# Moving the inversion of softmax sums, scaling out of PSUM, and finishing output blocks singly in a two-layer attention kernel

## The chip, the cores and the metric

The kernel runs on one core of a Trainium2 chip. The metric is the time of one execution on the device in microseconds (us). Before the change the median of three runs is 2982.2 us (2980.04 to 2982.8). The profile is of one further execution, with a span of 2983.8 us from its first instruction to its last. Five engines work side by side and wait for each other through semaphores: TensorE (PE; its weight loads are shown as PEld), VectorE (DVE), ScalarE (ACT), GpSimd (POOL), and SyncE (SP), which only issues DMA transfers here.

## What is computed

The input x is (8, 512, 32, 32) float32: eight batches of 512 channels and 1024 tokens. Two attention layers follow each other, cut here to what matters:

```python
# layer 0: layer norm, 8 heads of 64 channels, softmax, output projection, residual
xn  = layer_norm(x_flat)
q, k, v = xn @ Wq.T + bq, xn @ Wk.T + bk, xn @ Wv.T + bv          # split in 8 heads
attn = softmax(einsum('bqhd,bkhd->bhqk', q, k) / 8)
out = einsum('bhqk,bkhd->bqhd', attn, v) @ Wo.T + bo + x_flat
# layer 1: group norm (32 groups), one head of 512 channels, projection, residual
h = group_norm(x)
attn = softmax(einsum('bcn,bcm->bnm', q, k) * 512 ** -0.5)         # q, k, v from h
x + einsum('oc,bcn->bon', wp, einsum('bnm,bcm->bcn', attn, v)) + bp
```

The kernel leaves out the subtraction of the maximum in the softmax. It takes exponentials of the raw scores, adds them, and divides the values by the sums afterwards. A check of all sums at the end decides whether a second, general path is run; it is not for these inputs.

## The kernel before

Layer 0 works in pairs of heads for 512 of the queries: 8 pairs a batch. For each pair, TensorE makes scores for 8 tiles of 128 keys, ScalarE takes their exponentials p, VectorE adds the tiles to a sum, and TensorE multiplies p by the values. The scores of pair i+1 are always issued before the values of pair i. [...] Small pieces of work for VectorE and ScalarE are put in a queue by `later`, and `tick` takes one piece out at a time, once per key tile in `values`.

```python
def scores(self, ms):                       # class Pair
    for m in ms:
        s = wide_psum(f"s_{self.tag}_{m}")  # three such buffers
        ...  # two matmuls, one for each head                             (L681)
        nc.scalar.activation(p, s, AF.Exp, scale=1.0 / float(D) ** 0.5)  # (L684)
        ...  # self.sum = p[0] + p[1], then self.sum += p                (L688, L690)

def values(self):
    acc = bank(f"acc_{self.tag}")           # two such banks
    for m in range(NM):
        ...  # two matmuls, one for each head                             (L696)
        tick()
    nc.scalar.copy(self.o, acc)             # (L699)

def end_pairs(two):
    den = bank(f"den_{two[0].tag}")
    for k in range(4):                      # sums over keys               (L705)
        nc.tensor.matmul(den[ts(k, BL), :], ones[:, :BL], two[k // 2].sum[:, ts(k % 2, HB)],
                         start=True, stop=True)
    ...
    def invert():                           # transpose L489, reciprocal L655, check L659
        invert_sums(r, compact(t, den))
    def copies():                           # eight small copies to rows   (L718)
        ...  # nc.scalar.copy(rr[n][...], r[...])
    def scale(n):
        nc.vector.tensor_mul(two[n].o, two[n].o, rden[n])               # (L721)
    later(invert, copies)
    for n in range(2):
        later(lambda n=n: expand(rden[n], rr[n]))                        # (L494)
        later(lambda n=n: scale(n))
```

The loop over pairs, and what follows it (`more` is false in the last batch):

```python
for i, p in enumerate(pairs):
    if i + 1 < len(pairs):
        pairs[i + 1].scores(range(NM))
    ...
    p.values()
    if i in (2, 4, 6):
        end_pairs(pairs[i - 2 : i])
if more:
    k_units, kn = project(f"k{b + 1}", ...)     # keys of the next batch
    k_units[0].step(3)
end_pairs(pairs[-2:])
tick(2)
if more:
    k_units[0].rest()
...
o_units, x1 = project_out(b, wo_now, ob, stats)  # output projection, x_out, y_out, z_out
o_units[0].step(1)
add_operands(ob)                                 # T_o: differences of blocks of o
```

All large products are done block by block in seven multiplications instead of eight. Class `Product` has the seven steps. They accumulate into x, y and z in PSUM; S and T are sums and differences of blocks of the operands. A block that is complete is put in `behind`, and `finish` calls `after` for it:

```python
STEPS = [("11", "11", "x", True), ("12", "21", "z", True), ("S2", "T2", "x", False), ("S1", "T1", "y", True),
         ("S3", "T3", "x", False), ("22", "T4", "z", True), ("S4", "22", "y", False)]
...
        elif i == 1: self.out(0, 0, self.u1, self.z)       # out: VectorE adds u and PSUM (L341)
        elif i == 4: ...  # block (1, 1)
        elif i == 5: ...  # block (1, 0)
        elif i == 6: self.out(0, 1, self.u2, self.y)
        if i in (2, 4, 6):
            self.finish()
```

For the last product of layer 1 (x_o, y_o, z_o), `after` starts the load of the residual, scales, adds and stores:

```python
nc.sync.dma_start(out=xr, in_=self.x1[i, k][:, ts(r, HB)])                             # x1r
nc.vector.tensor_mul(t, t, self.rden[:, ts(k, HB)])                                    # (L860)
nc.vector.scalar_tensor_tensor(t, t, bm[:, oc : oc + 1], xr, ALU.add, ALU.add)         # (L861)
nc.sync.dma_start(out=out[b, ts(oc, P), ts(k, HB)], in_=t)                             # (L862)
```

Of the kernel before, what the change touches and what calls it, by code (L numbers as in the profile page):

```python
# [66 lines left out]
def fast_path(ctx: ExitStack, tc: tile.TileContext, x: bass.AP, vecs: dict, weights: dict, out: bass.AP,  # L67
# [41 lines left out]
    def bank(name):  # L109
        return ps_a.tile([P, HB], F32, tag="a", name=name)  # L110
# [196 lines left out]


    side = deque()

    def later(*work):
        side.extend(work)
# [6 lines left out]
    def until(done):  # L319
        while not done():  # L320
            side.popleft()()
# [5 lines left out]
    class Product:  # L327
# [4 lines left out]
        def __init__(self, tag, a, b, part, shift, dest, banks, after=None):  # L332
            self.tag, self.a, self.b, self.part, self.shift, self.dest = tag, a, b, part, shift, dest
            self.banks = banks
            self.after = after or (lambda i, k: None)
            self.behind = []
            self.pieces = 1
            self.done = 0

        def out(self, i, k, u, ps):  # L340
# [8 lines left out]
        def step(self, n=1):  # L349
            for _ in range(n):  # L350
                i = self.done
                self.done += 1
                a, b, to, opens = STEPS[i]
                until(lambda: a in self.a and b in self.b)
                if opens and not hasattr(self, to):
                    setattr(self, to, self.banks(to))
                self.part(getattr(self, to), self.a[a], self.b[b], opens)
                tick(self.pieces)
                if i == 0:
                    self.u1 = self.copy((0, 0))  # L360
                elif i == 1:
                    self.out(0, 0, self.u1, self.z)
                elif i == 2:
                    self.u2 = self.copy((0, 1))
                elif i == 4:
                    u3 = self.copy((1, 1))
                    self.out(1, 1, u3, self.y)
                    self.u3 = u3
                elif i == 5:
                    if self.shift.twice:  # L370
                        self.u3 = self.copy((1, 0))
                    self.out(1, 0, self.u3, self.z)
                elif i == 6:
                    self.out(0, 1, self.u2, self.y)
                if i in (2, 4, 6):
                    self.finish()

        def finish(self):
# [52 lines left out]
    def plain_shift():  # L431
        return make_shift(lambda u, ps, which: nc.scalar.copy(u, ps))  # L432
# [59 lines left out]
    def expand(t, r):  # L492

        nc.vector.transpose(t.rearrange("p (k i) -> p k i", i=BL), r.unsqueeze(2).to_broadcast((P, r.shape[1], BL)))  # L494
# [167 lines left out]
    class Pair:  # L662


        def __init__(self, b, hf, c, qt, kt, vt, ot):
            self.tag = f"{b}_{hf}_{c}"
            self.hf, self.c, self.vt = hf, c, vt
            self.q = qt[c // 2, hf][:, c % 2, :]
            self.k = [kt[c // 2, k][:, c % 2, :] for k in range(NH)]
            self.p = {}  # L670
            self.sum = None
            if c % 2 == 0:
                ot[c // 2, hf] = block(f"o_{self.tag}")
            self.o = ot[c // 2, hf][:, c % 2, :]

        def scores(self, ms):
            for m in ms:
                s = wide_psum(f"s_{self.tag}_{m}")
                for i in range(2):
                    r = slice(i * D, (i + 1) * D)  # L680
                    nc.tensor.matmul(s[:, ts(i, HB)], self.k[m // 4][r, ts(m % 4, P)], self.q[r, :],  # L681
                                     start=True, stop=True)
                p = big_tile(f"p_{self.tag}_{m}")
                nc.scalar.activation(p, s, AF.Exp, scale=1.0 / float(D) ** 0.5)  # L684
                self.p[m] = p
                if m == 1:
                    self.sum = big_tile(f"sum_{self.tag}")
                    nc.vector.tensor_add(self.sum, self.p[0], p)  # L688
                elif m > 1:
                    nc.vector.tensor_add(self.sum, self.sum, p)  # L690

        def values(self):
            acc = bank(f"acc_{self.tag}")
            for m in range(NM):
                for i in range(2):
                    nc.tensor.matmul(acc[i * D : (i + 1) * D, :], value_of(self.vt, m, self.c * P + i * D, D),  # L696
                                     self.p[m][:, ts(i, HB)], start=(m == 0), stop=(m == NM - 1))
                tick()
            nc.scalar.copy(self.o, acc)  # L699

    def end_pairs(two):

        den = bank(f"den_{two[0].tag}")
        for k in range(4):
            nc.tensor.matmul(den[ts(k, BL), :], ones[:, :BL], two[k // 2].sum[:, ts(k % 2, HB)],  # L705
                             start=True, stop=True)
        t = half_tile(f"dent_{two[0].tag}")
        r = small.tile([P, HB // BL], F32, tag="r", name=f"r_{two[0].tag}")
        rr = [small.tile([P, HB // BL], F32, tag=f"rr{n}", name=f"rr_{pair.tag}") for n, pair in enumerate(two)]
        rden = [half_tile(f"rden_{pair.tag}") for pair in two]  # L710

        def invert():
            invert_sums(r, compact(t, den))

        def copies():
            for n in range(2):
                for j in range(4):
                    nc.scalar.copy(rr[n][ts(j, BL), :], r[ts(2 * n + j // 2, BL), :])  # L718

        def scale(n):  # L720
            nc.vector.tensor_mul(two[n].o, two[n].o, rden[n])  # L721

        later(invert, copies)
        for n in range(2):
            later(lambda n=n: expand(rden[n], rr[n]))
            later(lambda n=n: scale(n))

    def project_out(b, w, ot, stats):

# [22 lines left out]
    class Whole:  # L752
# [90 lines left out]
        def values(self, v):  # L843
            b = self.b
            w = {f"{i + 1}{j + 1}": v[i, j].rearrange("p (m o) -> p m o", o=CB) for i in range(2) for j in range(2)}
            shared = {}

            def unit(r):
                y = {}

                def dest(i, k):
                    if (i, k) not in y:
                        y[i, k] = half_tile(f"y_{b}_{r}_{i}{k}")
                    return y[i, k]

                def after(i, k):
                    t, oc = dest(i, k), 2 * i + r
                    xr = half_tile(f"x1r_{b}_{k}_{oc}")
                    nc.sync.dma_start(out=xr, in_=self.x1[i, k][:, ts(r, HB)])
                    nc.vector.tensor_mul(t, t, self.rden[:, ts(k, HB)])  # L860
                    nc.vector.scalar_tensor_tensor(t, t, bm[:, oc : oc + 1], xr, ALU.add, ALU.add)  # L861
                    nc.sync.dma_start(out=out[b, ts(oc, P), ts(k, HB)], in_=t)  # L862

                return Product(f"o1_{b}_{r}", w, self.p, value_part(r), plain_shift(), dest,
                               banks_of(f"o1_{b}", r, shared), after)

            for n in SLOTS[3:]:
                sum_later(w, n, lambda n: big_tile(f"{n}_vm_{b}").rearrange("p (m o) -> p m o", o=CB), wide)
            return [unit(r) for r in range(2)]

    def all_checks():

        one = small.tile([P, 1], F32, tag="one", name="one")
        nc.vector.tensor_reduce(one, checks[:, : n_checks[0]], mybir.AxisListType.X, ALU.add)
        ps = bank("ps_check")
        nc.tensor.matmul(ps[:, :1], ones, one, start=True, stop=True)
        ok = small.tile([P, 1], F32, tag="ok", name="ok")
        nc.vector.tensor_scalar(ok, ps[:, :1], SUM_LIMIT, None, ALU.is_le)
        nc.vector.tensor_scalar(flag, ok[:1, :], -1.0, 1.0, ALU.mult, ALU.add)


    def bias_of(n):
# [2 lines left out]
    with tc.manual_schedule(engines=ORDERED):  # L885
# [67 lines left out]
        for b in range(B):  # L953
# [7 lines left out]
            for i, p in enumerate(pairs):  # L961
# [10 lines left out]
                    hb = operands(ln.result())  # L972
                    add_operands(hb)
                p.values()
                if i in (2, 4, 6):
                    end_pairs(pairs[i - 2 : i])
            if more:
                k_units, kn = project(f"k{b + 1}", wk_next, bias_of("bk0"), hb, True)
                k_units[0].step(3)
            end_pairs(pairs[-2:])  # L980
            tick(2)
            if more:
                k_units[0].rest()
            wa_now = load_w("a", b)
            ob = operands(ot)
# [40 lines left out]
            until(lambda: whole.summed)  # L1026
            whole.inverse()
            v_units[1].rest()
            if not more:
                all_checks()  # L1030
            if more:
                wv_next, wq_next = load_w("v", b + 1), load_w("q", b + 1)
            o_units = whole.values(vm)
            for u in o_units:
                u.step(2)
            for u in o_units:
                u.rest()
            until(lambda: not side)
# [389 lines left out]
```

## Time and profile before

| what | value |
| --- | --- |
| median of three runs | 2982.2 us |
| span of the profiled execution | 2983.8 us |
| mean granted TensorE clock | 0.995 of full speed |
| exponentials of layer 0 (L684) | 512 x 1054 ns on ScalarE |
| adds to the sums (L690) | 384 x 1225 ns on VectorE |
| copies of acc (L699) | 64 x 586 ns on ScalarE |
| copies to rows (L718) | 256 x 202 ns on ScalarE |
| expanding transposes (L494) | 64 x 708 ns on VectorE |
| scaling of o (L721) | 64 x 690 ns on VectorE |

A group's mean is the time of one instruction alone[...]. The "idle before" of a group is time in which its engine had nothing to do just ahead of such an instruction, and the name behind the arrow is what ended it. Idle time of an engine that bounds nothing costs nothing. Ends of matmuls are modelled, so the starts of the instructions say more of TensorE than its busy share does. An "x32" in the chain counts passes of matmuls and weight loads, not matmuls of the program.

### The profile page before, as it was taken

The numbers are of one execution on the slowest core, as the hardware profiler recorded it, in microseconds if no ns is written. First come the engines' busy times: TensorE is split into PE (matmuls) and PEld (weight loads), VectorE is DVE, ScalarE is ACT, GpSimd is POOL, SyncE is SP. The second block draws the span as 40 slices with busy tenths as digits, with TensorE's granted clock in tenths as the row PEclk, the third lists the DMA queues.
The fourth block names the chain that finished last, engine by engine and source line by source line (L and its number), as shares of the span: only waits on it lengthen the run. The fifth ranks groups of instructions, "written<-read, shape, count | busy, mean of one in ns | idle before, by whom it ended". The sixth has DMA issues, their size and how long they took to land.

```text
span 2983.8 us, 26676 instructions
## 1 busy us (share of the span) xinstructions
PE 2956.7 (99%) x10043; PEld 1374.4 (46%) x10043; DVE 1777.3 (60%) x2266; ACT 1047.1 (35%) x1649; POOL 22.0 (1%) x37
## 2 busy tenths in 40 slices
PE   9999999999999999999999999999999999999898
PEld 4533455345543455334553345533455334553344
DVE  6667446665467654676546755567556675446644
ACT  3462215612165121551226412263223632135220
POOL 2000000000000000000000000000000000000000
PEclk9999999999999999999999999999999999999899
DMA  8103130031300322012310123102131031301201
GB/s 296 50 25 127 46 124 25 25 134 42 120 25 28 132 69 94 25 57 102 110 53 25 60 99 116 47 25 81 79 120 43 25 109 50 110 25 53 78 1 58
DMA packets 84921, 217.33 MB, mean 73 GB/s; under 512 B 8704, under 2 KB 12848, under 8 KB 84784
## 3 DMA queue, kind: packets, MB, share of 16 engines
q1 hardware_dynamic: 81616, 204.51, 19.8%
q0 software_dynamic: 3072, 11.01, 1.0%
q8 instruction: 81, 1.33, 0.2%
q14 instruction: 56, 0.46, 0.1%
q10 hardware_dynamic: 96, 0.02, 0.0%
HBM read 156.26 MB, written 59.24 MB: 72 GB/s over the span
## 4 chain that ended last, share of the span: by engine, by line
PE 97%; DVE 2%; DMA 1%; issue 0%; ACT 0%; SPq 0%; DVEq 0%
PE s L681 15%; PE acc L696 15%; PE x_o L427 6%; PE x_s L419 6%; PE y_s L419 4%; PE y_o L427 4%; PE z_s L419 4%; PE z_o L427 4%; PE x_q L402 3%; PE x_k L402 3%; PE x_qa L402 3%; PE x_vm L411 3%; PE x_v L411 3%; PE x_out L402 2%; PE y_k L402 2%; PE y_q L402 2%
## 5 line engine op out<-in xcount | busy, mean ns | idle before, releaser
L684 ACT ACTIVATE p<-s 128x1024 f32<-128x1024 f32 x512 | 476.3, 1054 | 85.1 <-PE s L681 85.1
L690 DVE TENSOR_TENSOR sum<-sum,p 128x1024 f32<-128x1024 f32 x384 | 470.5, 1225 | 40.7 <-DVE sum L690 0.9
L696 PE MATMUL acc<-p,v 128*64 128x512 f32 x2048 | 453.6, 595 | 0.0
L681 PE MATMUL s<-q,k_again 64*128 64x512 f32 x1792 | 402.9, 599 | 0.0
L696 PEld LDWEIGHTS acc<-p,v 128*64 128x64 f32 x2048 | 141.4, 137 | 305.0 <-issue 292.2
L681 PEld LDWEIGHTS s<-q,k_again 64*128 64x128 f32 x1792 | 161.6, 185 | 240.0 <-ACT p L684 119.4
L688 DVE TENSOR_TENSOR sum<-p,p 128x1024 f32<-128x1024 f32 x64 | 78.4, 1225 | 200.9 <-ACT p L684 200.9
L419 PE MATMUL x_s<-S_qa,T_gn 128*128 128x512 f32 x256 | 120.3, 592 | 0.0
L427 PE MATMUL x_o<-T_p,S_vm 128*128 128x512 f32 x256 | 115.1, 592 | 0.0
L699 ACT COPY o<-acc 128x512 f32<-128x512 f32 x64 | 37.5, 586 | 217.3 <-PE acc L696 216.9
L781 ACT ACTIVATE p<-p 128x512 f32<-128x512 f32 x128 | 80.7, 630 | 73.1 <-DVE p L341 73.1
L341 DVE TENSOR_TENSOR p<-u(1, 1)_s,y_s 128x512 f32<-128x512 f32 x32 | 22.0, 689 | 132.3 <-ACT u(1, 1)_s L432 132.3
L718 ACT COPY rr<-r 32x16 f32<-32x16 f32 x256 | 51.6, 202 | 101.8 <-DVE r L655 98.8
L449 ACT ACTIVATE u(0, 0)_k<-x_k,vecs 128x512 f32<-128x512 f32 x16 | 11.0, 687 | 214.7 <-PE x_k L402 214.7
L494 DVE STREAM_TRANSPOSE rden<-rr 128x512 f32<-128x512 f32 (+1 forms) x72 | 55.3, 768 | 36.9 <-ACT rr L718 23.3
L419 PEld LDWEIGHTS x_s<-S_qa,T_gn 128*128 128x128 f32 x256 | 48.6, 190 | 61.2 <-issue 61.0
L427 PEld LDWEIGHTS x_o<-T_p,S_vm 128*128 128x128 f32 x256 | 48.6, 190 | 61.2 <-issue 61.2
L341 DVE TENSOR_TENSOR y<-u(1, 1)_o,y_o 128x512 f32<-128x512 f32 x16 | 11.0, 688 | 108.7 <-ACT u(1, 1)_o L432 108.7
L402 PE MATMUL x_out<-T_o,w_o 128*128 128x512 f32 x128 | 62.0, 608 | 3.2 <-DVE T_o L481 3.2
L411 PE MATMUL x_vm<-w_m,T_gn 128*128 128x256 f32 x256 | 60.5, 379 | 0.0
L419 PE MATMUL y_s<-S_qa,gn 128*128 128x512 f32 x128 | 60.2, 593 | 0.0
L419 PE MATMUL x_s<-qa,gn 128*128 128x512 f32 x128 | 60.1, 592 | 0.0
(320 smaller groups left out, 4396.3 us busy)
## 6 DMA issues: line engine op xcount, KB each, us to landing
x<-in_x_dram SPq DMA_DIRECT2D x32, 512.0 KB, 7.5
xr<-in_x_dram SPq DMA_DIRECT2D x64, 256.0 KB, 2.7
x_away<-x SPq DMA_DIRECT2D x32, 512.0 KB
x1r<-x_away SPq DMA_DIRECT2D x64, 256.0 KB, 3.1
out_dram<-y SPq DMA_DIRECT2D x64, 256.0 KB, 2.3
k_away<-k SPq DMA_DIRECT2D x28, 512.0 KB, 2.6
k_again<-k_away SPq DMA_DIRECT2D x28, 512.0 KB
w_o<-saved_o SPq DMA_DIRECT2D x24, 512.0 KB, 4.1
```

The lines of the kernel that those rows point to most:

```text
L402: nc.tensor.matmul(dst, a[:, k, ts(r, P)], b[:, k, :], start=(opens and k == 0), stop=(k == 1), skip_group_check=True)
L411: nc.tensor.matmul(dst[:, ts(m, CB)], b[:, k, ts(2 * r + m, P)], a[:, k, :], start=(opens and m == 0 and k == 0), stop=(k == 1), skip_grou ...
L419: nc.tensor.matmul(dst, b[:, k, ts(r, P)], a[:, k, :], start=(opens and k == 0), stop=(k == 1), skip_group_check=True)
L427: nc.tensor.matmul(dst, a[:, m, ts(r, P)], b[m // 2][:, m % 2, :], start=(opens and m == 0), stop=(m == NM // 2 - 1), skip_group_check=True)
L494: nc.vector.transpose(t.rearrange("p (k i) -> p k i", i=BL), r.unsqueeze(2).to_broadcast((P, r.shape[1], BL)))
L681: nc.tensor.matmul(s[:, ts(i, HB)], self.k[m // 4][r, ts(m % 4, P)], self.q[r, :], start=True, stop=True)
L684: nc.scalar.activation(p, s, AF.Exp, scale=1.0 / float(D) ** 0.5)
L688: nc.vector.tensor_add(self.sum, self.p[0], p)
L690: nc.vector.tensor_add(self.sum, self.sum, p)
L696: nc.tensor.matmul(acc[i * D : (i + 1) * D, :], value_of(self.vt, m, self.c * P + i * D, D), self.p[m][:, ts(i, HB)], start=(m == 0), stop ...
L718: nc.scalar.copy(rr[n][ts(j, BL), :], r[ts(2 * n + j // 2, BL), :])
L781: nc.scalar.activation(dest(i, k), dest(i, k), AF.Exp, scale=float(C) ** -0.5)
```

## The change

It has four parts.

1. The sums of two pairs are taken across keys (`den`) directly behind the values of the first of them, and inverted on VectorE in the middle of the next scores. Before, this was done behind the values of the next pair but one. The reciprocals are then there when the second pair's values are done.
2. The second pair's values are multiplied by their reciprocals as they leave PSUM, on VectorE, instead of being copied by ScalarE and scaled later. The first pair's are copied and then scaled as before.
3. The blocks of the last product are finished singly, each as soon as it is complete.
4. The check of the sums at the end of the last batch is split in two and put between steps of that batch's last product.

```diff
@@ class Product
+            self.at_once = False
...
-                if i in (2, 4, 6):
+                if i in (2, 4, 6) or self.at_once:
                     self.finish()
@@ class Pair, scores
+                if m == 4:
+                    while at_scores:
+                        at_scores.pop()()
@@ class Pair, values
-            nc.scalar.copy(self.o, acc)
+            if self.c % 2 == 0:
+                nc.scalar.copy(self.o, acc)
+            else:
+                until(lambda: self.rden is not None)
+                nc.vector.tensor_mul(self.o, acc, self.rden)
@@ end_pairs, now invert_pairs
-        def scale(n):
-            nc.vector.tensor_mul(two[n].o, two[n].o, rden[n])
-        later(invert, copies)
-        for n in range(2):
-            later(lambda n=n: expand(rden[n], rr[n]))
-            later(lambda n=n: scale(n))
+        def rows(n):
+            expand(rden[n], rr[n])
+            two[n].rden = rden[n]
+        at_scores.append(invert)
+        later(lambda: [at_scores.pop()() for _ in list(at_scores)], copies, lambda: rows(1), lambda: rows(0),
+              lambda: nc.vector.tensor_mul(two[0].o, two[0].o, rden[0]))
@@ last product of layer 1
+                u.at_once = True
@@ all_checks
         nc.vector.tensor_reduce(one, ...)
+        yield
         ...  # matmul, comparison, flag
+        yield
@@ the loop over pairs
                 p.values()
-                if i in (2, 4, 6):
-                    end_pairs(pairs[i - 2 : i])
+                if i % 2 == 0:
+                    invert_pairs(pairs[i : i + 2])
             if more:
                 k_units, kn = project(f"k{b + 1}", ...)
-                k_units[0].step(3)
-            end_pairs(pairs[-2:])
-            tick(2)
-            if more:
                 k_units[0].rest()
@@ the last product
-            if not more:
-                all_checks()
...
+            check = iter(()) if more else all_checks()
             for u in o_units:
                 u.step(2)
+                next(check, None)
```

Cut here: the initialisation of `at_scores` and `rden`.

More of the change, by code (lines that the diff above doesn't have):

```diff
@@ L309, in fast_path @@
     side = deque()
+    at_scores = []
     def later(*work):
@@ L670, in __init__ @@
             self.p = {}
-            self.sum = None
+            self.sum = self.rden = None
             if c % 2 == 0:
@@ L698, in values, with invert_pairs @@
                 tick()
-            nc.scalar.copy(self.o, acc)
-    def end_pairs(two):
+            if self.c % 2 == 0:
[3 more added lines that the diff above has]
+                nc.vector.tensor_mul(self.o, acc, self.rden)
+    def invert_pairs(two):
         den = bank(f"den_{two[0].tag}")
@@ L862, in after @@
                     nc.sync.dma_start(out=out[b, ts(oc, P), ts(k, HB)], in_=t)
-                return Product(f"o1_{b}_{r}", w, self.p, value_part(r), plain_shift(), dest,
-                               banks_of(f"o1_{b}", r, shared), after)
+                u = Product(f"o1_{b}_{r}", w, self.p, value_part(r), plain_shift(), dest,
+                            banks_of(f"o1_{b}", r, shared), after)
+                u.at_once = True
+                return u
             for n in SLOTS[3:]:
```

## The prediction

> **What bounds the kernel now.** I read the share of busy time first, then the chain that ended last, and then timelines of the places where that chain leaves TensorE. In the busy table each engine has its time, its share of the span and its instructions; under it is the head of the chain.
>
> ```profile
> PE 2956.7 (99%) x10043; PEld 1374.4 (46%) x10043; DVE 1777.3 (60%) x2266; ACT 1047.1 (35%) x1649; POOL 22.0 (1%) x37
> ...
> PE 97%; DVE 2%; DMA 1%; issue 0%; ACT 0%; SPq 0%; DVEq 0%
> ```
>
> TensorE is the bound nearly everywhere, so VectorE or ScalarE work saved beside it is worth nothing in itself. Only four things are: a wait of TensorE, a slow clock of it, a switch of its matmul shapes, and the tail after its last matmul. So I looked for those. Next, the chain in order of time in the seventh of eight batches (start, duration, what):
>
> ```profile
> 2358.90 7.07 PE s L681 x32
> 2365.97 7.02 PE acc L696 x32
> 2372.99 7.23 PE s L681 x32
> ...
> 2402.32 7.35 PE s L681 x32
> ...
> 2428.32 1.72 PE x_k L402 x4
> 2430.04 1.00 PE den L705 x8
> 2431.04 1.91 PE y_k L402 x4
> 2432.95 1.72 PE x_k L402 x4
> ```
>
> Scores of a pair take 7.07 us, but twice in a batch 7.23 and 7.35. The sums of the last two pairs (den) stand between two steps of the key projection, and the step behind them takes 1.91 instead of 1.72. ScalarE's timeline at the first slow scores tells why (start, duration, instruction, in brackets the idle time before it and what ended it):
>
> ```profile
> 2372.13 1.71 ACT L718 COPY rr<-r 32x16 f32<-32x16 f32 x8 [4.68 <-DVE r L655]
> 2373.86 0.59 ACT L699 COPY o<-acc 128x512 f32<-128x512 f32 x1
> 2374.34 1.95 ACT L684 ACTIVATE p<-s 128x1024 f32<-128x1024 f32 x2
> ```
>
> The eight row copies wait for the reciprocals r, which VectorE makes only after all sums of those scores. The copy of acc, ready at 2373.0, and the first exponential, ready 1.2 us after its scores begin, stand behind them. Eight exponentials take 7.44 us for 7.07 us of scores, with three score buffers, so a late start reaches TensorE.
>
> The last batch has no key projection. TensorE's timeline there, then the windows view (window, length, PE busy, granted clock, DMA share, GB/s):
>
> ```profile
> 2785.71 1.07 PE L705 MATMUL den<-sum,ones 128*32 128x512 f32 x8
> 2786.70 1.98 PE L402 MATMUL x_out<-o,w_o 128*128 128x512 f32 x4
> ...
> 2797.01 3.78 PE L402 MATMUL x_out<-T_o,w_o 128*128 128x512 f32 x4 [3.17 <-DVE T_o L481]
> ```
>
> ```profile
> 2797.00:2804.00 7.00, 6.99 (x9) 0.56 0.97 329
> 2820.00:2832.00 12.00, 8.43 (x15) 0.57 0.11 43
> ```
>
> TensorE waits 3.17 us for T_o and then runs 7 us at about half clock. It falls to half clock a second time around the group norm at 2820. Last, VectorE at the very end:
>
> ```profile
> 2974.92 0.69 DVE L341 TENSOR_TENSOR y<-u(0, 1)_o,y_o 128x512 f32<-128x512 f32 x1 [2.75 <-PE y_o L427]
> 2975.53 0.69 DVE L860 TENSOR_TENSOR y<-y,rden 128x512 f32<-128x512 f32 x1
> 2976.25 0.75 DVE L861 SCALAR_TENSOR_TENSOR y<-y,bm,x1r 128x512 f32<-128x512 f32 x1
> 2976.91 0.68 DVE L860 TENSOR_TENSOR y<-y,rden 128x512 f32<-128x512 f32 x1
> 2977.64 0.75 DVE L861 SCALAR_TENSOR_TENSOR y<-y,bm,x1r 128x512 f32<-128x512 f32 x1
> ```
>
> Block (1,0), added at 2971.49, is finished only after the last block (0,1) was added.
>
> [...] In the groups, the multiply from SBUF (o<-o,rden) averages 690 ns and an add with a PSUM operand (y<-u(1, 1)_o,y_o) 688, so scaling out of PSUM costs VectorE no more.
>
> **The change part by part.**
> (1) The sums of pairs i, i+1 (i even) move from behind the values of i+2 to behind those of i. Their number stays four per batch, so their 1.0 us each stays on TensorE. They need the sum of pair i+1. In the second pair of the seventh batch its last VectorE add ends at 2327.93 and the values end at 2329.67: 1.7 us to spare.
> (2) The inversion (0.71 + 0.25 + 0.19 + 0.09, about 1.25 us) stands after the fifth tile's add in the scores of i+2. In the third pair's timeline that add ends at 2338.0, which is 1.3 us into the values that follow (2336.7), so r is ready about 2.4 us into them. The row copies then run where ScalarE is idle, and nothing stands behind them before the next scores. This takes away the slow starts: (7.23 - 7.07) + (7.35 - 7.07) = 0.44 us a batch, over 8 batches 3.5 us.
> (3) Odd pairs lose the ScalarE copy (32 x 586 ns, hidden) and VectorE multiplies straight from PSUM. I chose the third pair of batch seven as the tight place: its adds now end at 2342.0, 5.3 us into its values (from 2336.7). Delayed by 1.25 us they end at 6.5, two transposes (0.74 each) and two multiplies (0.69 each) at 9.4, and the next scores' first add starts at 2346.96, or 10.2. 0.8 us to spare, and a slip would meet the 1.7 us of (1).
> (4) In seven batches the sums leave the key projection: 1.91 - 1.72 = 0.19 us of switching each, 1.3 us. The values-to-projection switch was there before.
> (5) In the last batch the fourth sums precede the last values, the last pair is scaled in 0.7 us, and T_o is ready in time, as in batch seven, whose output projection takes 2438.15 to 2462.99 = 24.8 us, or 25.0 with a first step of 1.91. In the last it takes 2786.78 to 2817.73 = 31.0. Gain 6.0 us, in which the wait (3.2) and the half clock (about 3.3) are both counted, less a 0.4 us wait for a residual DMA that batch seven has.
> (6) The check of the sums moves between steps of the last product: TensorE's wait of 0.97 us for its reduction goes.
> (7) Finishing each block at once puts one multiply and one add with residual (2976.25 to 2977.64) before the last block's add: 1.4 us off the tail. In the other batches these operations stay beside TensorE. The SP queue's order changes: the next batch's key and input loads stand behind the first outputs, so the inputs start near 2226 instead of 2208 in batch seven, but the first use is at 2261.7.
>
> Sum: 3.5 + 1.3 + 6.0 + 1.0 + 1.4 = 13.2 us. 2982.2 - 13.2 = 2969.0.
>
> **The rivals.** First, a new wait in place of the old: the sums behind the values of i wait for VectorE, or the accumulation's bank is held until rden is there. For it: VectorE has more in line between scores and values, and margins are 0.8 and 1.7 us. Against it: the bank is next used a whole pair later. A slip of 0.5 us in 32 places would cost 16 us and make it about 2985. Second, the loads pushed back in the SP queue meet the residual reads and hold VectorE, and through the half-size buffers ScalarE and TensorE. For it: 4 MB move into the product's stage. Against it: the copy that is waited for has some 2.6 us until TensorE needs it. A microsecond in each of seven batches would leave about 2976. Third, only the one-off parts act (5 to 7), with the slow scores staying because ScalarE itself limits them: 2982.2 - 8.4 = 2973.8. Against it, unhindered scores show 7.07 with the same exponentials.
>
> **Range and chances.** [...] the three runs differ by 2.8 us. Small new waits would cost a few us more, while little can bring more gain. I take 2963 to 2976. A gain of 13 us is 0.45%, far from 2% either way: within 2% has 0.98, slower 0.015, faster 0.005.
>
> **What would show it.** Right: all scores near 7.07 us in the chain, TensorE's wait for T_o and the low clock near 2797 gone, while the second stretch stays; no den between x_k and y_k; the tail with three VectorE operations after the last matmul instead of five. Wrong: idle of den on a VectorE sum, of scores or values on a scaling multiply, or a first layer norm add that waits for an input load.

## The result and the profile after

The changed kernel took 2967.59 us in the median of four runs (2967.15 to 2969.4), the kernel before 2982.17 (2980.04 to 2982.8). The ratio is 0.9954 with a 95% interval of 0.9936 to 0.9971. In a later series, five runs gave 2969.21 against 2981.24, a ratio of 0.9957 (0.9943 to 0.9970). The gain was 14.6 us at first and 12.0 in that later series, for 13.2 predicted.

The busy line of TensorE and the head of the chain hardly move, as the chain is TensorE's own work in both kernels:

```profile
PE 2945.7 (99%) x10043; PEld 1378.4 (46%) x10043; DVE 1773.6 (60%) x2266; ACT 1030.9 (35%) x1617; POOL 22.1 (1%) x37
...
PE 97%; DVE 1%; DMA 1%; issue 0%; ACT 0%; SPq 0%; DVEq 0%
```

ScalarE has 32 instructions less, the copies of the second pairs. The chain in order of time in batch seven (start, duration, what) shows where the first gain came from:

```profile
2354.54 7.07 PE s L683 x32
2361.61 7.02 PE acc L701 x32
2368.62 7.07 PE s L683 x32
...
2397.79 7.07 PE s L683 x32
...
2423.52 1.72 PE x_k L404 x4
2425.24 1.72 PE y_k L404 x4
```

The scores that took 7.23 and 7.35 us take 7.07, no den stands between x_k and y_k, and y_k is back at 1.72. ScalarE in the second and fourth pair's values of that batch (start, duration, instruction, idle before it):

```profile
2334.61 1.71 ACT L728 COPY rr<-r 32x16 f32<-32x16 f32 x8 [0.69 <-DVE r L657]
2336.35 2.23 ACT L575 ACTIVATE x<-x,vecs 128x512 f32<-128x512 f32 x3
2340.63 3.77 ACT L686 ACTIVATE p<-s 128x1024 f32<-128x1024 f32 x4 [2.05 <-PE s L683]
...
2363.89 1.71 ACT L728 COPY rr<-r 32x16 f32<-32x16 f32 x8 [0.75 <-DVE r L657]
2369.73 2.85 ACT L686 ACTIVATE p<-s 128x1024 f32<-128x1024 f32 x3 [4.13 <-PE s L683]
```

The row copies now come early, and the exponentials behind them wait for TensorE's scores, not the other way round. In the second pair's values, three activations of the next batch's layer norm stand between them; they end 2 us before the exponentials.

TensorE's timeline in the last batch, and then the windows view (window, length, busy time of PE, PEld, DVE, ACT and POOL, granted clock, DMA share, GB/s) around T_o and around the group norm:

```profile
2772.61 7.09 PE L701 MATMUL acc<-p,v 128*64 128x512 f32 x32
2779.62 1.98 PE L404 MATMUL x_out<-o,w_o 128*128 128x512 f32 x4
...
2786.59 1.88 PE L404 MATMUL x_out<-T_o,w_o 128*128 128x512 f32 x4
```

```profile
2786.00:2798.00 12.00, 11.87 (x28) 5.05 (x27) 9.22 (x13) 0.00 (x0) 0.00 (x0) 1.00 0.76 265
2806.00:2818.00 12.00, 7.73 (x13) 3.70 (x14) 7.56 (x23) 2.67 (x5) 0.00 (x0) 0.57 0.17 67
```

T_o is in time, with no idle before its first product, and the clock is full. The group norm's stretch is still at 0.57. At the very end, VectorE has three operations behind the last matmul instead of five:

```profile
2960.47 0.69 DVE L343 TENSOR_TENSOR y<-u(0, 1)_o,y_o 128x512 f32<-128x512 f32 x1 [1.23 <-PE y_o L429]
2961.19 0.69 DVE L870 TENSOR_TENSOR y<-y,rden 128x512 f32<-128x512 f32 x1
2961.92 0.75 DVE L871 SCALAR_TENSOR_TENSOR y<-y,bm,x1r 128x512 f32<-128x512 f32 x1
```

Starts of matmuls, taken as differences, split the time of the two profiled executions (us). Each stage runs from the first matmul of its kind to the first of the next:

| stage | before | after | difference |
| --- | --- | --- | --- |
| start to first scores | 116.59 | 114.82 | -1.77 |
| first scores to output projection, batches 1 to 7, each | 141.74 to 141.78 | 141.10 to 141.18 | -0.64 |
| the same, last batch | 129.43 | 128.92 | -0.51 |
| output projection to group norm, batches 1 to 7, mean | 28.01 | 27.96 | -0.05 |
| the same, last batch | 33.41 | 27.19 | -6.22 |
| group norm to layer 1 scores, last batch | 31.67 | 31.73 | +0.06 |
| layer 1 scores to last product, last batch | 74.79 | 73.44 | -1.35 |
| last product to the end | 57.23 | 55.72 | -1.51 |

### The profile page after: what moved, and what is told of

Same layout as the page of the kernel before. It is cut to its first block, busy times and chain, and to the rows that moved or that the text cites. A ratio compares the mean times of both kernels' runs of the same rounds, so it can differ in the third digit from the quotient of the medians.

```text
span 2967.7 us, 26543 instructions
## 1 busy us (share of the span) xinstructions
PE 2945.7 (99%) x10043; PEld 1378.4 (46%) x10043; DVE 1773.6 (60%) x2266; ACT 1030.9 (35%) x1617; POOL 22.1 (1%) x37
## 4 chain that ended last, share of the span: by engine, by line
PE 97%; DVE 1%; DMA 1%; issue 0%; ACT 0%; SPq 0%; DVEq 0%
PE s L683 15%; PE acc L701 15%; PE x_o L429 6%; PE x_s L421 6%; PE y_s L421 4%; PE y_o L429 4%; PE z_o L429 4%; PE z_s L421 4%; PE x_q L404 3%; PE x_k L404 3%; PE x_vm L413 3%; PE x_qa L404 3%; PE x_v L413 3%; PE x_out L404 2%; PE y_q L404 2%; PE z_qa L404 2%
## 5 line engine op out<-in xcount | busy, mean ns | idle before, releaser
L705 ACT COPY o<-acc 128x512 f32<-128x512 f32 x32 | 18.8, 586 | 155.3 <-PE acc L701 155.3
L343 DVE TENSOR_TENSOR qa<-u(1, 1)_qa,y_qa 128x512 f32<-128x512 f32 x16 | 11.0, 688 | 82.4 <-ACT u(1, 1)_qa L451 82.4
L421 PE MATMUL y_s<-S_qa,T_gn 128*128 128x512 f32 x128 | 60.1, 592 | 0.0
```

The costliest lines, as they stand in the source:

```text
L421: nc.tensor.matmul(dst, b[:, k, ts(r, P)], a[:, k, :], start=(opens and k == 0), stop=(k == 1), skip_group_check=True)
```

## The experiments

The two theories that matter: mine was that the row copies' lateness on ScalarE made the slow scores (A1), and that T_o's wait together with the half clock behind it cost 6 us (A2). The rivals were that scaling out of PSUM brought the gain (B), and that the low clock or the tail had other causes (C). All medians below stand beside runs of the kernel before in the same series: 2982.26 us in the first, 2982.17 in the second, 2981.24 in the third.

**The tail alone.** The kernel before with these two edits:

```diff
+                u.at_once = True
-            if not more:
-                all_checks()
+            check = iter(()) if more else all_checks()
+                next(check, None)    # between steps of the last product
```

> The kernel before with only the blocks of the last product finished singly and the check of the sums split (parts 3 and 4 of the change). Theory: these two act only at the end of the last batch, 1.3 us from TensorE's wait for the check and 1.5 us from the tail, so about 2.8 us less than before: near 2979.4, with the slow scores (7.23, 7.35) and the 3.2 us wait for T_o still there. Rival A, that finishing singly also helps or hurts in the other seven batches through the order of the loads: a difference of the seven batches in the trace of more than 0.3 us each.

Measured: 2980.59 us, ratio 0.9992 (0.9984 to 1.0000), or 1.7 us less. In the trace, the stage before the last product is 73.44 instead of 74.79 us and the end 55.74 instead of 57.23. TensorE's wait for the check is gone; before, it was (us in total, times, longest):

```profile
PE ps_check L876 <- DVE one L874: 1.0, 1, 1.0
```

The attention stage of the other seven batches is the same within 0.04 us in five of them. In the fifth it is 0.35 us longer, with a third slow score, and in the seventh 0.22 longer, so nothing is gained there. Both parts act only at the end. The median shows less than the trace. Over all profiles, the last stage took 56.5 to 57.3 us in four without single finishing and 55.7 to 56.2 in nine with it: about 1.0 us.

**The inversion alone.** The changed kernel without those two edits.

> The changed kernel without single finishing and with the check in one piece where it was (parts 1 and 2 alone). Theory: 5.3 us in eight batches and 6.2 us in the last batch's output projection stay, so about 11.5 us less than before: near 2970.7, and together with the run that has only the tail the parts add up to the whole within 1 us. Rival A: the parts help each other, and the two savings add up to clearly less or more than 14.6 us.

Measured: 2971.38 us, ratio 0.9965 (0.9952 to 0.9979), 10.9 us less. Its trace has the changed kernel's 141.10 us in the attention stage and 27.04 in the last output projection, and at the end 74.79 and 57.26 us, like the kernel before. Together with the tail 12.6 us, 2 us short of the 14.6 first measured and outside the 1 us I allowed, but near the 12.0 of the later series. Nothing here shows that the parts need each other.

**Copy instead of scaling out of PSUM.**

```diff
             else:
                 until(lambda: self.rden is not None)
-                nc.vector.tensor_mul(self.o, acc, self.rden)
+                nc.scalar.copy(self.o, acc)
+                nc.vector.tensor_mul(self.o, self.o, self.rden)
```

> The changed kernel, but the second pair's values are copied by ScalarE and then scaled from SBUF by VectorE, as the first pair's are; the inversion stays in the middle of the next scores. Theory: the row copies end about 4.1 us into the values, 2.9 us before the copy of acc is ready, so the copy (0.6 us) is done before the first exponential (1.2 us into the scores): no slow scores, time equal to the changed kernel within 1 us. Rival B, that scaling out of PSUM is what removed the slow scores: 7.2 to 7.35 us comes back in two or three scores of a batch, 3.5 to 6 us in all.

Measured: 2968.12 us, ratio 0.9953 (0.9939 to 0.9966), and 141.10 or 141.11 us in the seven batches' attention stage, for 141.10 to 141.18 in the changed kernel. Rival B falls: with the early inversion, scaling out of PSUM brings nothing measurable.

**Late inversion and copy.** The same, and

```diff
-                if m == 4:
+                if m == NM - 1:
```

> As the run before this one, and the inversion stands behind the last add of the next scores instead of the fifth. Theory: r comes 6.3 us into the values, the row copies end at about 8.05, the copy of acc at 8.6, so the first exponential starts about 0.4 us late and three scores of a batch (the fourth, sixth and eighth) take 0.15 to 0.3 us longer: 4 to 7 us more than the changed kernel, near 2973. Rival B', that the slow scores had another cause in the old order (the place of the sums on TensorE): scores stay at 7.07 and the time stays near 2967.6.

Measured: 2989.19 us, ratio 1.0024 (1.0015 to 1.0032): 21.6 us more than the changed kernel's 2967.59, or 20.0 more than 2969.21, where I expected 4 to 7. The direction was right and the size far off. ScalarE's timeline in batch seven, and then TensorE's at the fourth pair's scores, show why:

```profile
2356.76 1.71 ACT L729 COPY rr<-r 32x16 f32<-32x16 f32 x8 [4.68 <-DVE r L657]
2358.49 2.22 ACT L575 ACTIVATE x<-x,vecs 128x512 f32<-128x512 f32 x3
2360.62 0.56 ACT L708 COPY o<-acc 128x512 f32<-128x512 f32 x1
2361.09 7.41 ACT L686 ACTIVATE p<-s 128x1024 f32<-128x1024 f32 x8
```

```profile
2357.55 2.85 PE L683 MATMUL s<-q,k_again 64*128 64x512 f32 x12
2362.15 4.79 PE L683 MATMUL s<-q,k_again 64*128 64x512 f32 x20 [1.76 <-ACT p L686]
```

I had left out the three layer norm activations in the line behind the row copies. They push the first exponential to 3.5 us after the start of its scores, instead of 1.2, and after six of sixteen matmuls (x12 are passes) TensorE stands still for lack of a score buffer. This happens in seven batches, which take 143.91 us instead of 141.10. In the last one, which has no next layer norm, the stage takes 0.67 us longer than in the changed kernel. The chain there has the slow scores of the kernel before again, and one more: 7.23, 7.35 and 7.29 us for the fourth, sixth and eighth pair, 0.66 us in all over 7.07. So where only the copy of acc stands behind the row copies, the expected 0.15 to 0.3 us a score was right. Nothing but the place of the inversion differs from the run above, which has none of it.

**Late inversion with scaling out of PSUM.** Only the second edit.

> The changed kernel with scaling out of PSUM kept, but the inversion behind the last add of the next scores. Theory, after the run that was late and copied: the row copies end 8 us into the second pair's values, and three activations of the next batch's layer norm (2.2 us) stand behind them on ScalarE, so the fourth pair's first exponential comes about 1.5 to 2 us late in seven batches, and nowhere else, as there is no copy of acc: 8 to 12 us more than the changed kernel, near 2977, with the sixth and eighth scores at 7.07. Rival B: scaling out of PSUM shields the scores whatever the place of the inversion: 2967.6 within 1 us.

Measured: 2981.56 us, ratio 0.9997 (0.9988 to 1.0005); 14.0 us more than the changed kernel's 2967.59 and 12.3 more than 2969.21, above the 8 to 12 that I expected. The attention stages of the two traces differ by 12.4 us. The attention stage took 142.85 to 142.93 us in seven batches and 128.92, as in the changed kernel, in the last. ScalarE's timeline in batch seven, and then in the last batch:

```profile
2349.82 1.70 ACT L728 COPY rr<-r 32x16 f32<-32x16 f32 x8 [4.68 <-DVE r L657]
2351.55 2.22 ACT L575 ACTIVATE x<-x,vecs 128x512 f32<-128x512 f32 x3
2353.68 2.82 ACT L686 ACTIVATE p<-s 128x1024 f32<-128x1024 f32 x3
```

```profile
2711.84 1.71 ACT L728 COPY rr<-r 32x16 f32<-32x16 f32 x8 [4.68 <-DVE r L657]
2713.80 7.44 ACT L686 ACTIVATE p<-s 128x1024 f32<-128x1024 f32 x8 [0.26 <-PE s L683]
```

With the copy of acc gone, only the layer norm activations are left in the way. In the last batch the row copies are as late as in the kernel before (6.2 us into the values), but the first exponential behind them still waits for its scores. So scaling out of PSUM does protect the scores where nothing else stands in the line; the seven other batches show that it is not enough.

**The old kernel with later row copies.** It moves the row copies of two of the four groups out of the way. The two transposes and two scalings on VectorE that are queued behind them move too:

```diff
-        later(invert, copies)
+        later(invert, *[nothing] * wait, copies)    # wait is 8 for the first two groups
```

> The kernel before, with eight empty pieces put between the inversion and the row copies of the first two groups of pairs, so that the copies run at the start of the next values, where their reciprocals have long been there. Nothing else is moved. Theory: the slow scores (7.23 and 7.35 in each of eight batches) become 7.07: 3.5 us less than before, near 2978.7. Rival B', that they come from the sums on TensorE ahead of the scores before, or from VectorE: no change, 2982.2.

Measured: 2979.14 us, ratio 0.9990 (0.9981 to 0.9998), 3.0 us less than before. The attention stage took 141.30 us in six of the first seven batches, 0.44 to 0.48 less than before, 141.54 in the fifth, and 128.93 in the last, 0.50 less. All scores of batch seven take 7.07; these are the two that were slow:

```profile
2368.13 7.07 PE s L681 x32
...
2397.30 7.07 PE s L681 x32
```

A1 is shown, with its size. That VectorE's four pieces did it, which moved along ("nothing else is moved" was wrong), is ruled out by the last batch of the run before: they are late there too, the next scores' first add even starts behind them, and no score is slow. What slowed the scores was ScalarE's line: late row copies with the copy of acc and the first exponential behind them.

**Keeping TensorE busy in the wait for T_o.** The kernel before, and in the last batch

```diff
+            if not more:
+                keep_busy("busy", 3)    # 12 matmuls of 128 columns on constants
```

> The kernel before, with three groups of extra matmuls (2.6 us, on constants, into a free bank, read by nobody) where TensorE waits 3.2 us for T_o in the last batch. Theory: the wait is no shorter, but the clock stays full, and the 6.8 us at half clock behind it go: 3.3 us less than before, near 2978.9, with the group norm's stretch still at half clock. Rival C: the slow matmuls there come from something else, such as transfers (the DMA share is 0.97 there), and the time stays near 2982.2 or grows.

Measured: 2981.73 us, ratio 0.9999 (0.9991 to 1.0007). In the profiled execution it did what A2 says: the wait shrank to 0.5 us behind the extra work, the clock stayed at 1.00, and the output projection to group norm took 30.34 us instead of 33.41. But the median moved by only 0.4 us, with an interval from 2.7 us less to 2.1 more. Two readings stay open. One is that many runs of the kernel before do not have the full half clock of its profile: of 57 runs of it in the first two series, seven had a mean clock of 0.995 like the profiled one, and took 2985.8 us on average; 25 had 0.998, and took 2981.2. With the extra matmuls 11 of 13 runs had 0.998. The other is that part of the gain is lost elsewhere: in batches 1 to 7 of this profile TensorE waits 2.2 us for y_out, for 1.0 in the profile of the kernel before.

**The last batch as before.** The changed kernel, with the last two pairs of the last batch handled in the old order and by copy.

> The changed kernel with the last pair of pairs of the last batch alone done as before: sums behind the last values, copy by ScalarE, scaling from SBUF behind it. Theory: the wait of 3.2 us for T_o comes back, and with it, [...] 6.8 us at half clock: 2.9 us more than the changed kernel in a run without the half clock, 6.2 with it, so 3 to 5 in the median and a wider spread. Rival D: the wait comes back but costs 6 us in every run, as the prediction's sum counted it.

Measured: 2974.01 us, ratio 0.9976 (0.9966 to 0.9986), 4.8 us more than the changed kernel beside it, as expected of the median. TensorE's timeline:

```profile
2789.51 2.56 PE L404 MATMUL x_out<-T_o,w_o 128*128 128x512 f32 x4 [3.17 <-DVE T_o L483]
2791.87 3.04 PE L404 MATMUL y_out<-T_o,w_o 128*128 128x512 f32 x4
2794.75 1.88 PE L404 MATMUL x_out<-T_o,w_o 128*128 128x512 f32 x4
```

The wait is 3.17 us as before. Starts tell the half clock here: y_out starts 2.36 us after x_out and the next x_out 2.88 after that, for 1.72 each at full clock. That is 1.8 us lost. In the profile of before, the steps behind the x_out at 2797.01 were:

```profile
2800.59 3.18 PE L402 MATMUL y_out<-T_o,w_o 128*128 128x512 f32 x4
2803.60 1.88 PE L402 MATMUL x_out<-T_o,w_o 128*128 128x512 f32 x4
```

By the same count they took 3.58 and 3.01 us and lost 3.15. The profiles of the tail alone and of the later row copies, which keep the old order here, lost 3.0 and 2.9. Rival D, 6 us in every run, does not fit a median of 4.8. But the spread did not widen as I expected either (2973.04 to 2975.58).

**Keeping TensorE busy in the group norm.** The changed kernel with extra matmuls before each of three dependent steps of the last batch's group norm, run twice.

> The changed kernel with such extra matmuls in the last batch's group norm (1.7, 0.9 and 2.6 us before its three dependent TensorE steps). Theory: the second stretch at half clock (some 6.5 us of work from the first query product on) goes, 2.5 to 3.2 us less than the changed kernel, near 2964.7. Rival C: the extra matmuls delay the group norm's own small ones and nothing is won: 2967.6 or more.

> The changed kernel once more, unaltered, on the same chip as the two runs behind it, as their measure, and to learn how far its time moves from run to run. Expected: 2967.5 to 2969.5. If it comes near 2970, part of the first measured gain of 14.6 us was the draw of the runs.

> The changed kernel with extra matmuls in the last batch's group norm, as before, now beside the changed kernel on the same chip. In its first trace the stretch from the group norm to the first scores took 28.48 us instead of 31.73, but its median was not lower. Theory: 1.5 to 3.2 us less than the changed kernel here, as that stretch takes 30.1 to 31.7 without the extra matmuls. Rival C: no difference, as something gives the gain back elsewhere.

Measured: 2968.00 us at first (0.9955, 0.9941 to 0.9968), and then 2968.20 beside 2969.21 for the changed kernel (0.9954, 0.9941 to 0.9968). Windows view of the second:

```profile
2806.00:2818.00 12.00, 11.41 (x65) 8.31 (x64) 10.08 (x27) 2.67 (x5) 0.00 (x0) 1.00 0.28 111
```

The clock is full, and the stretch from the group norm to the scores takes 28.48 us, against 30.70 and 31.73 in the changed kernel's two profiles. But the time is only 1.0 us lower and the intervals overlap, so I do not call it faster. The rest is given back elsewhere: over the eight batches, TensorE waits for y_out 3.6 and 3.2 us in the two traces, instead of 1.2 in each of the changed kernel's. VectorE's waits for the loads of the residual xr are longer too, 20.1 and 19.5 us for 11.6 and 11.5. That they are the cause is not shown: in the run with the copy they are 17.8 us, with 1.1 for y_out. The run with extra matmuls in the wait for T_o showed the same (2.2 instead of 1.0). Why TensorE waits longer in kernels that differ only in the last batch, stays open.

## Why the prediction was right, step by step

The mechanism held. The sum came near in part by luck: the term of the last batch was too large for the median run, two small terms were off by 0.4 us each in opposite directions, and the 14.6 us first measured hold some 2.5 us that no part explains.

- **(1) Sums early.** Right. TensorE never waits for a sum at den.
- **(2) and (4), slow scores and switching.** Predicted 0.44 + 0.19 = 0.63 us a batch, measured 0.64 in seven batches; in the last, which has no switching term, 0.44 predicted and 0.51 measured. The cause of the first term is shown by the later row copies (0.44 to 0.50) and by the late inversion with the copy, which brings the slow scores back. The switching term was seen only in the chain, not isolated; the 0.20 us that separate the later row copies (141.30) from the changed kernel (141.10) have its size. The statement that nothing stands behind the row copies was wrong: layer norm activations do, and the step held only because the copies come early enough.
- **(3) VectorE's margin.** Right: in batch seven the last multiply ended 8.7 us into the second pair's values (2332.44 to 2341.14), for 9.4 expected, and the next add began 1.5 us later, for 0.8 expected.
- **(5) Last batch.** The mechanism was right and the size too large for the median run. I counted 6.0 us, with 3.3 of half clock from the profile; in the pair of profiles the stage differs by 6.2, but put back by itself the old order costs 4.8 in the median. The wait of 3.2 us is in every profile with the old order and no extra work; the half clock behind it varies. I had also compared 3.78 us, a duration, with 1.72, a time from start to start; by starts the step took 3.58. How much half clock the median run pays is not settled: the run with extra matmuls moved by 0.4 us, with an interval much wider than that, the 4.8 us leave 1.6 beside the wait, and the four profiles with the wait show 1.8 to 3.15.
- **(6) and (7).** Predicted 0.97 and 1.4 us, measured 1.35 in the pair of traces, and about 1.0 over all profiles for the tail.

Measured terms: 7 x 0.64 + 0.51 + 4.8 + 1.35 + 1.0 = 12.1 us, beside the 12.0 us of the third series, where the changed kernel was run again. The further 2.5 us of the first measurement are not explained by any part. The start alone differs by 1.77 us between the two profiles: in the windows from 30 to 42 us the granted clock is 0.86 before and 1.00 after. That is the draw of an execution, as the changed kernel's own second profile takes 115.74 us to the first scores. The rival of a new wait did not happen: no wait of TensorE is new in the changed kernel. The rival of pushed-back loads happened in its first half: batch seven's input loads start 69 us before its first scores instead of 88, and VectorE waits 15.9 us for the residual x1r over the whole run instead of 10.6 (16.3 in the run with the tail alone and 10.8 with the inversion alone, so it comes with single finishing). But TensorE does not feel it: the time from the last product to the next scores of batches 2 to 7 is 86.95 us in both.

## What to carry to other kernels

Ask of each waiting instruction not how long it takes but what stands behind it on its engine. In the kernel before, ScalarE's copy of acc was ready at 2373.0 us and started at 2373.86, behind the row copies. Eight copies of 0.2 us cost TensorE 0.44 us a batch with one copy and an exponential behind them, and 1.8 to 2.8 where layer norm work was queued behind them as well. Moving the producer earlier cured this; moving the copy of acc off the engine cured it only where nothing else was in the line. And before a clock dip of one profile goes into a sum, look at the granted clock of several runs: here it was 0.995 in seven of 57 and 0.998 in 25.

## What the runs showed of the hardware

**Clock behind the wait for T_o.** The stretch at half clock behind one and the same wait of 3.2 us cost 3.15, 3.0 and 2.9 us in three executions and 1.8 in a fourth. In the window from 2790 to 2804 us the granted clock was 0.76 in the first three. It was 1.00 there in the changed kernel, which does not wait for T_o, and 1.00 from 2790 to 2800 us in the run with extra matmuls, where 0.5 us of the wait was left.

**Clock in the group norm.** With the same idle times of TensorE in it (2.4, 0.8 and 2.6 us), the stretch took from 30.08 to 31.73 us in eleven profiles. In the two with extra matmuls it took 28.48. This draw of 1.65 us is larger than several parts of this change. What decides how much of such a stretch runs at half clock was not shown.

**VectorE and PSUM.** In the changed kernel the multiply out of PSUM (o<-acc,rden) took 685 ns on average and the one from SBUF (o<-o,rden) 693, each 32 times at 128x512.

**Rows of instructions on ScalarE.** In the kernel before, eight exponentials of 1054 ns on average took 7.45 us in a row, less than their sum of 8.43; eight row copies of 202 ns took 1.71, a little more than their sum of 1.62.
